# A graph network in three layers on one core: node parts stored by even and odd tiles, and the last group's store issued later

## The chip, the cores and the metric

The kernel runs on one core of one Trainium2 chip. The core has five engines with a queue of instructions each: PE multiplies matrices, DVE, ACT and POOL compute on vectors, SP issues transfers. SBUF is the on-chip memory of 128 partitions, PSUM takes the matmul results, DRAM is the memory outside. The metric is the device time of one execution in microseconds (us); where several runs are shown, their median.

## The reference

2,500 nodes carry 256 numbers each; 80,000 edges, sorted by `dst`, join them. The input is normalised row by row and clipped at zero, and then three edge convolutions follow, each

```python
m = concat([h[dst], h[src] - h[dst]]) @ W + b      # one row for each edge
s = segment_sum(m, dst); cnt = edges that end in the node
h = relu(s / max(cnt, 1))
```

The output is `x + concat([h0, h1, h2, h3]) @ Wf + bf`.

## The kernel before

The sum over edges is turned into a product with a matrix of counts. With `Wt` and `Wb` the upper and lower half of `W`, the sum for a node is `cnt * h @ (Wt - Wb)` plus the sum of `z = h @ Wb` over the sources of its edges. So each layer first makes `z`, 20 tiles of 128 nodes, and then multiplies it with the count matrix `a`, whose rows are source nodes and whose columns are destination nodes.

`z` is kept in two parts, `zh` (rounded to the matmul's fp32r format) and `zl` (the rest), so that two fast matmuls give the product nearly in fp32. Both lie in SBUF as `[128, 20, 256]`: tile `t` starts 1,024 bytes after tile `t - 1`, so all tiles of a part have the same address modulo 256. In the built program `zh` starts at byte 57504 and `zl` at byte 77984 of a partition, both 160 modulo 256.

The destinations are cut into five groups: four of 480 columns and one of 468 (`GWS`, in windows of 6). A group's slice of `a` is `[128, 20, n]` fp32r, in one of two buffers in turn (`apools`), at bytes 151200 and 189600, again 160 modulo 256. A row of 480 columns is 1,920 bytes, seven and a half times 256, so rows of even tiles start at 160 modulo 256 and rows of odd tiles at 32. A row of 468 columns is 1,872 bytes, so those starts move by 80 from tile to tile.

`layer(l, g, a, own)` is the inner loop. For each tile `i` it issues four matmuls: output half 0 with `zh` and `zl`, output half 1 with `zh` and `zl`. The 128 x 128 piece of `z` is the stationary operand (the weights, loaded anew for each matmul) and the row `a[:, i, :n]` is streamed. Four more matmuls add `hT` times `Wt - Wb` (L966).

Layer 0 (called with `PEo`, so its matmuls carry the helper's line L280) also builds `a`, group by group: DVE compares keys (`one_m`, `one_n`), PE counts, ACT copies the counts into the next group's `a`. Each of the first four groups is stored to DRAM by `store_a` (`finish`), as the later layers need it again. The fifth stays in SBUF for layer 1, and is stored after layer 1's nodes in the source text, but on the queue object `SP`, which leaves the place in SP's stream to the tile scheduler. `SPo`, `PEo`, `DVEo`, `ACTo` and `POOLo` are the same engines with program order kept. Layers 1 and 2 read the groups back with `load_a`; layer 1 walks the groups from the last to the first.

56 edges of the few nodes left over from the windows are not in `a`. Their rows of `z` are fetched from DRAM by indirect transfers that POOL issues: in layer 0 by `gather` (accumulating into `sums`), in later layers by `gather_pairs` (into spare buffers `one_m`, added by DVE). For this the nodes go to `z_dram`: in layer 0 by `keep_nodes`, `zh` first from SP, then `zl` added on from POOL, for five ranges of tiles; in later layers by `nodes_split`, tile by tile. `layer_few` closes each layer: it needs the sum of the fetched rows (`add_sums`).

`split_high`, `split_low` and `nodes_split` write `zh` and `zl`; `keep_nodes`, `layer` and `layer_few` read them.

Of the kernel before, what the change touches and what calls it, by code (L numbers as in the profile page):

```python
# [8 lines left out]
F32 = mybir.dt.float32  # L9
I32 = mybir.dt.int32  # L10
AF = mybir.ActivationFunctionType
OP = mybir.AluOpType
# [253 lines left out]
F32R = mybir.dt.float32r  # L266
# [45 lines left out]
def by_windows(ctx: ExitStack, tc: tile.TileContext, x, src, dst, Ws, bs, Wf, bf, out, missing):  # L312
    nc = tc.nc
    PE, DVE, ACT, POOL, SP = nc.tensor, nc.vector, nc.scalar, nc.gpsimd, nc.sync
    PEo, DVEo, POOLo, ACTo, SPo = (InOrder(tc, e) for e in (PE, DVE, POOL, ACT, SP))
    P = 128
    N, D = x.shape
    E = src.shape[0]
    NT = (N + P - 1) // P
# [9 lines left out]
    FEW = 112  # L329
# [18 lines left out]
    NG = len(GWS)  # L348
    Q = NT // 2
# [9 lines left out]
    const = ctx.enter_context(tc.tile_pool(name="const", bufs=1))  # L359
# [9 lines left out]
    def bank():  # L369
        return ps[-1].tile([P, 512], F32, name="bank")  # L370
# [1 line left out]

    acc = const.tile([P, NT, D], F32, name="acc")
    hT = const.tile([P, DC, NP], F32, name="hT")
    zh = const.tile([P, NT, D], F32R, name="zh")
    zl = const.tile([P, NT, D], F32R, name="zl")
    key_m = const.tile([P, NW, CH, REP], BF16, name="key_m")
    key_n = const.tile([P, NW, CH, REP], BF16, name="key_n")
    away = const.tile([P, WG, CAP], BF16, name="away")
# [16 lines left out]
    z_dram = [dram.tile([NP, D], F32, name=f"z_dram{l}") for l in range(L)]  # L396
# [3 lines left out]
    cnt_few = const.tile([P, FEW], F32R, name="cnt_few")  # L400
    mine = const.tile([P, W], F32, name="mine")
    most = const.tile([P, 1], F32, name="most")
    a_dram = [dram.tile([P, NT, n * W], F32, name=f"a_dram{g}") for g, n in enumerate(GWS)]
# [5 lines left out]

    shift = pp.tile([P, P + 1], F32, name="shift")  # L410
    ident = shift[:, :P]


    dst_rows = dst.rearrange("(p c) -> p c", p=P)
# [17 lines left out]
    def load_wb(l, queue=SP):  # L432
        ws[l] = wpool.tile([P, DC, D], F32, name="wt"), wpool.tile([P, DC, D], F32, name="wb", bufs=1)
        queue.dma_start(ws[l][1], Ws[l][D:2 * D, :].rearrange("(c p) d -> p c d", p=P))
# [29 lines left out]
    def load_b(l, queue=SP):  # L464
        queue.dma_start(brow[PAD:PAD + 1, l % 2, :], bs[l].rearrange("(o d) -> o d", o=1))
# [262 lines left out]
    zf0 = pp.tile([P, D], F32, name="zf0")  # L728
# [5 lines left out]
    def split_high(q):  # L734
        t, p = 2 * q, pz[q, False]
        if q == Q - 1:
            ACTo.copy(zh[:, t, :], p[:, :D])
            ACTo.copy(zh[:, t + 1, :], zf0)
        else:
            ACTo.copy(zh[:, t:t + 2, :], p.rearrange("p (i d) -> p i d", i=2))  # L740

    def split_low(q):
        t, p = 2 * q, pz.pop((q, False))
        if q == Q - 1:
            DVEo.tensor_sub(zl[:, t, :], p[:, :D], zh[:, t, :].bitcast(F32))
            DVEo.tensor_sub(zl[:, t + 1, :], zf0, zh[:, t + 1, :].bitcast(F32))
        else:
            DVEo.tensor_sub(zl[:, t:t + 2, :], p.rearrange("p (i d) -> p i d", i=2),
                            zh[:, t:t + 2, :].bitcast(F32))

    def first_final(q):
        ACTo.copy(acc[:, 2 * q:2 * q + 2, :], pz.pop((q, True)).rearrange("p (i d) -> p i d", i=2))
# [1 line left out]
    def nodes_split(l, t, zf):  # L754
        pz = bank()
        for c in range(DC):
            PE.matmul(pz[:, :D], hT[:, c, t * P:(t + 1) * P], ws[l][1][:, c, :],  # L757
                      start=(c == 0), stop=(c == DC - 1))
        sc = share[:, t:t + 1]
        if t == NT - 1:  # L760
            DVEo.scalar_tensor_tensor(zf, pz[:, :D], sc, brow[:, l % 2, :], op0=OP.mult, op1=OP.add)
        else:
            ACT.activation(zf, pz[:, :D], AF.Copy, scale=sc)
        SPo.dma_start(z_dram[l][t * P:(t + 1) * P, :], zf)
        DVEo.tensor_copy(zh[:, t, :], zf)
        DVEo.tensor_sub(zl[:, t, :], zf, zh[:, t, :].bitcast(F32))

    def add_rest(ts):

# [19 lines left out]
    def group_of(g):  # L789
        return FEW + sum(GWS[:g]) * W, GWS[g] * W  # L790

    def touched(g):
        c0, n = group_of(g)
        return [t for t in range(NT) if (t + 1) * P > c0 and t * P < c0 + n]

    def new_a(g):

        n = group_of(g)[1]
        a = apools[g % 2].tile([P, NT * GS], F32R, name="a")
        return a[:, :NT * n].rearrange("p (t n) -> p t n", n=n)  # L800
# [53 lines left out]
            store_a(g, a)  # L854
        yield

    def store_a(g, a):
        for t in range(0, NT, 5):
            SP.dma_start(a_dram[g][:, t:t + 5, :], a[:, t:t + 5, :].bitcast(F32))

    def load_a(g):
        a = new_a(g)
# [9 lines left out]

    def keep_nodes(l, a, b):

        to = z_dram[l][a * P:b * P, :].rearrange("(k p) d -> p k d", p=P)
        SPo.dma_start(to, zh[:, a:b, :].bitcast(F32))
        yield
        POOLo.dma_start(to, zl[:, a:b, :].bitcast(F32), accum_op=OP.add)

    def gather(l):  # L880

# [16 lines left out]
    def rooms(l):  # L898

        for _ in range(AHEAD):  # L900
            two = room()
            yield two[:, 0, :]
            yield two[:, 1, :]
        for i in range(SUMS):
            yield sums[:, i, :]
        for _ in range(AHEAD):
            yield hot.tile([P, BW * CH, NB], BF16, name="one_n", bufs=AHEAD).rearrange(
                "p k m -> p (k m)")[:, :2 * D].bitcast(F32)
# [24 lines left out]
    def layer_few(l):  # L933
        pa = ps_agg.tile([P, DC, 512], F32, name="pa")
        for o in range(DC):
            for c in range(DC):
                PEo.matmul(pa[:, o, :FEW], ws[l][0][:, c, o * P:(o + 1) * P], hT[:, c, :FEW],
                           start=(c == 0), stop=False)
            for z in (zh, zl):
                PEo.matmul(pa[:, o, :FEW], z[:, NT - 1, o * P:(o + 1) * P], cnt_few, start=False, stop=False)  # L940
            PEo.matmul(pa[:, o, :FEW], sums[:, 0, o * P:(o + 1) * P], only, start=False, stop=True)
        ACTo.activation(hT[:, :, :FEW], pa[:, :, :FEW], AF.Relu)

    unit = [None]

    def layer(l, g, a, own, PE=PE, ACT=ACT):

        c0, n = group_of(g)
        pa = ps_agg.tile([P, DC, 512], F32, name="pa")
        ways = [(o, c) for o in range(DC) for c in range(DC)]  # L950
        units = [(0, k) for k in range(NT)]
        for i, u in enumerate(own):
            units.insert(u + i, (1, i))
        last = {}
        for kind, i in units:
            last.update({o: (kind, i, o) for o in (range(DC) if kind == 0 else ways[i][:1])})
        for kind, i in units:
            if kind == 0:
                for o in range(DC):
                    for z in (zh, zl):  # L960
                        unit[0] = PE.matmul(pa[:, o, :n], z[:, i, o * P:(o + 1) * P], a[:, i, :n],  # L961
                                            start=(i == 0 and z is zh),
                                            stop=(z is zl and last[o] == (kind, i, o)))
            else:
                o, c = ways[i]
                unit[0] = PE.matmul(pa[:, o, :n], ws[l][0][:, c, o * P:(o + 1) * P], hT[:, c, c0:c0 + n],  # L966
                                    start=False, stop=(last[o] == (kind, i, o)))
            yield
        ACT.activation(hT[:, :, c0:c0 + n], pa[:, :, :n], AF.Relu)  # L969
# [8 lines left out]
    a = new_a(0)  # L978
# [55 lines left out]
    for g in range(NG):  # L1034
# [26 lines left out]
        if g + 1 < NG:  # L1061
            run(finish(g + 1, a1))
            held, a = a, a1
# [4 lines left out]
    tiles = {NG - 1: a, NG - 2: held}  # L1068
    for l in range(1, L):
        groups = list(range(NG))  # L1070
        if l % 2:
            groups.reverse()


        last = [t for t in touched(groups[0]) if t]
        for t, zf in zip([t for t in range(1, NT) if t not in last] + last + [0], rooms(l)):
            nodes_split(l, t, zf)
        if l == 1:

            store_a(NG - 1, tiles[NG - 1])  # L1080
        few = gather_pairs(l)
        next(few)
        if l + 1 < L:
            load_b(l + 1)
            load_wb(l + 1)
            load_wt(l + 1)
        finished = []
        for j, g in enumerate(groups):
            now = [t for t in touched(g) if t not in finished]
            for t in now:  # L1090
                final(l, t)
            finished += now
            rest = add_rest(now) if l == 1 else None
            if j == NG - 1:
                load_wf(l + 1)
            for u, _ in enumerate(layer(l, g, tiles[g], LATE)):
                if u % 4 == 1:
                    next(few, None)
                if rest and u in (1, NT):
                    next(rest, None)  # L1100
            if j == 1 and l + 1 < L:
                DVEo.tensor_sub(ws[l + 1][0], ws[l + 1][0], ws[l + 1][1])
            if j + 2 < NG:
                del tiles[g]
                tiles[groups[j + 2]] = load_a(groups[j + 2])
        run(few)
        add_sums(2)
        layer_few(l)
# [41 lines left out]
```

## Time and profile before

| | us |
|---|---|
| median of three runs | 512.57 (512.41 to 512.95) |
| the profiled execution | 510.9 |
| its span, first to last instruction | 509.1 |
| layer 0's matmuls with `a` | 61.0 to 199.9 |
| wait for the fetched rows, `layer_few` of layer 0 | PE idle 1.75 |
| layer 1's nodes begin | 206.8 |
| layer 2's nodes begin | 347.1 |
| last layer's output begins | 486.8 |

An engine's busy share is a mean over stages. Starts of matmuls are times at which the next one began, so the distance from one start to the next is what a matmul costs in a dense stream; the shown duration of one (some 0.38 us) overlaps the next.

### The profile page before, as it was taken

How to read it: one execution, taken by the hardware profiler on the slowest of the kernel's cores; microseconds unless marked ns; L12 is line 12 of the kernel's file. 1: busy time of each engine (PE TensorE's matmuls, PEld its weight loads, DVE VectorE, ACT ScalarE, POOL GpSimd, SP SyncE). 2: the span in 40 equal slices, each digit the busy share in tenths (PEclk: the TensorE clock that was granted, in tenths of full speed). 3: DMA queues.
4: the chain of work that ended last, by engine and by line, in shares of the span. 5: the costliest groups of instructions: out<-in, count | busy, mean ns of one | idle time of the engine just before them, and what ended most of it. 6: DMA issues, size and time to landing. Idle time of an engine off the chain costs nothing.

```text
span 509.1 us, 7543 instructions
## 1 busy us (share of the span) xinstructions
PE 498.3 (98%) x2875; PEld 410.4 (81%) x2875; DVE 262.4 (52%) x552; ACT 135.9 (27%) x310; POOL 250.2 (49%) x231
## 2 busy tenths in 40 slices
PE   8999999999999999899999999999999999999996
PEld 4898888778788887788687878788887878787885
DVE  7999988888897810782214240415812231213033
ACT  5676667744634310430000000004300000000010
POOL 3694218888888870007666573610176645451000
PEclk9999999999999999999999999999999999999999
DMA  9327987895959898343399999872335878898023
GB/s 277 95 71 135 227 275 242 281 232 163 324 87 363 124 169 306 112 138 94 114 379 338 300 242 285 82 131 85 123 106 196 354 242 279 236 257 84 1 89 119
DMA packets 41475, 98.72 MB, mean 194 GB/s; under 512 B 4999, under 2 KB 31574, under 8 KB 35798
## 3 DMA queue, kind: packets, MB, share of 16 engines
q1 hardware_dynamic: 22198, 68.78, 36.7%
q0 software_dynamic: 18304, 28.26, 32.5%
q10 hardware_dynamic: 928, 1.11, 0.7%
q8 instruction: 24, 0.39, 0.3%
q14 instruction: 21, 0.17, 0.1%
HBM read 60.63 MB, written 37.50 MB: 193 GB/s over the span
## 4 chain that ended last, share of the span: by engine, by line
PE 67%; POOL 19%; DMA 8%; issue 4%; DVE 1%; ACT 0%; DVEq 0%; POOLq 0%; SPq 0%; ACTq 0%
PE pa L961 34%; POOL sums L280 19%; PE bank L781 10%; PE bank L757 7%; PE pa L966 6%; PE pz L280 6%; DMA sums<-z_dram,who 3%; PE bank L280 2%; DMA wf<-in_L_gnn_Wf_dram 2%; DMA z_dram<-zl 1%; DMA z_dram<-zh 1%; PE pa L280 1%; DMA dst_i<-in_dst_dram 1%; PE turned L280 1%; DVE sums L280 0%
## 5 line engine op out<-in xcount | busy, mean ns | idle before, releaser
L280 POOL DMA_INDIRECT one_m<-z_dram,who x112 | 111.0, 991 | 153.2 <-DVE acc L280 40.5
L961 PE MATMUL pa<-a,zh 128*128 128x480 f32 (+1 forms) x400 | 152.8, 382 | 0.0
L961 PE MATMUL pa<-a,zl 128*128 128x480 f32 (+1 forms) x400 | 151.4, 378 | 0.0
L280 POOL DMA_INDIRECT sums<-z_dram,who x56 | 95.7, 1710 | 23.8 <-issue 16.8
L280 DVE TENSOR_TENSOR sums<-sums,one_m 128x512 f32<-128x512 f32 x52 | 36.0, 692 | 106.1 <-DMA one_m<-z_dram,who 104.2
L961 PEld LDWEIGHTS pa<-a,zl 128*128 128x128 f32 x400 | 75.1, 188 | 11.3
L961 PEld LDWEIGHTS pa<-a,zh 128*128 128x128 f32 x400 | 75.1, 188 | 11.0
L280 PE MATMUL pa<-a,zh 128*128 128x480 f32 (+1 forms) x200 | 81.5, 408 | 0.0
L280 DVE TENSOR_TENSOR one_m<-iota_m,key_m 128x1024 bf16<-128x1024 bf16 x100 | 68.6, 686 | 16.5 <-PE bank L280 14.4
L280 PE MATMUL pa<-a,zl 128*128 128x480 f32 (+1 forms) x200 | 75.7, 379 | 0.0
L969 ACT ACTIVATE hT<-pa 128x960 f32<-128x960 f32 (+1 forms) x10 | 9.7, 966 | 232.5 <-PE pa L966 205.0
L280 ACT CAST a<-bank 128x480 fp32r<-128x480 f32 x100 | 51.0, 564 | 59.1 <-PE bank L280 51.5
L280 DVE TENSOR_TENSOR one_n<-iota_n,key_n 128x960 bf16<-128x960 bf16 x100 | 65.0, 650 | 0.0
L280 DVE SCALAR_TENSOR_TENSOR acc<-bank,share,acc 128x256 f32<-128x256 f32 x60 | 28.7, 483 | 65.6 <-PE bank L781 59.1
L781 PE MATMUL bank<-wf,hT 128*128 128x256 f32 x240 | 54.0, 379 | 1.8 <-issue 1.3
L781 PEld LDWEIGHTS bank<-wf,hT 128*128 128x128 f32 x240 | 45.5, 190 | 11.4 <-issue 5.1
L280 PEld LDWEIGHTS <-one_m 128*128 128x128 bf16 x796 | 43.3, 98 | 8.6 <-issue 3.5
L280 PE MATMUL bank<-one_n,one_m 128*128 128x120 bf16 x796 | 48.9, 216 | 0.0
L280 PEld LDWEIGHTS pa<-a,zh 128*128 128x128 f32 x200 | 37.7, 188 | 8.4 <-issue 3.0
L280 PEld LDWEIGHTS pa<-a,zl 128*128 128x128 f32 x200 | 37.6, 188 | 7.0 <-issue 2.1
L757 PE MATMUL bank<-wb,hT 128*128 128x256 f32 x160 | 34.9, 379 | 0.0
L966 PE MATMUL pa<-hT,wt 128*128 128x480 f32 (+1 forms) x80 | 34.0, 565 | 0.1
(145 smaller groups left out, 413.1 us busy)
## 6 DMA issues: line engine op xcount, KB each, us to landing
a<-a_dram SPq DMA_DIRECT2D x20, 1200.0 KB
a_dram<-a SPq DMA_DIRECT2D x16, 1200.0 KB
a_dram<-a SPq DMA_DIRECT2D x4, 1170.0 KB
a<-a_dram SPq DMA_DIRECT2D x4, 1170.0 KB
out_dram<-acc SPq DMA_DIRECT2D x19, 128.0 KB
z_dram<-one_m SPq DMA_DIRECT2D x16, 128.0 KB
z_dram<-sums SPq DMA_DIRECT2D x16, 128.0 KB
acc<-in_x_dram POOLq DMA_DIRECT2D x4, 512.0 KB
```

The source lines that it names most:

```text
L280: return self.tc.keep_in_program_order(call(*args, **kwargs))
L757: PE.matmul(pz[:, :D], hT[:, c, t * P:(t + 1) * P], ws[l][1][:, c, :], start=(c == 0), stop=(c == DC - 1))
L781: PE.matmul(po[:, :D], hT[:, c, t * P:(t + 1) * P], wfs[l][:, c, :], start=(c == 0), stop=(c == DC - 1))
L961: unit[0] = PE.matmul(pa[:, o, :n], z[:, i, o * P:(o + 1) * P], a[:, i, :n], start=(i == 0 and z is zh), stop=(z is zl and last[o] == (kin ...
L966: unit[0] = PE.matmul(pa[:, o, :n], ws[l][0][:, c, o * P:(o + 1) * P], hT[:, c, c0:c0 + n], start=False, stop=(last[o] == (kind, i, o)))
L969: ACT.activation(hT[:, :, c0:c0 + n], pa[:, :, :n], AF.Relu)
```

## The change

Two edits.

`zh` and `zl` become `[128, 2, 2560 + 32]`: first the ten even tiles, then, after 32 floats (128 bytes) of room, the ten odd tiles. `tile_of` and `pair_of` find a tile, or tiles `2q` and `2q + 1`, in it. An even tile's weights start at 160 modulo 256 as before; an odd tile's start at 32. The tiles that follow in SBUF move by 512 bytes (`zl` by 256), which keeps them as they were modulo 256: the buffers of `a` start at 151712 and 190112. So in the groups of 480 columns the weights of a tile and the row that they are multiplied with start at the same address modulo 256, for even and for odd tiles. `keep_nodes` can't write both halves of a range in one transfer any more; ranges of more than two tiles go in two.

The store of the fifth group is issued on `SPo`, so that it stands in SP's stream where the text has it: behind the 20 node stores of layer 1 (the second of the three layers).

```diff
-    zh = const.tile([P, NT, D], F32R, name="zh")
-    zl = const.tile([P, NT, D], F32R, name="zl")
+    zh = const.tile([P, 2, Q * D + 32], F32R, name="zh")
+    zl = const.tile([P, 2, Q * D + 32], F32R, name="zl")
...
+    def tile_of(z, t):
+        return z[:, t % 2, t // 2 * D:(t // 2 + 1) * D]
+
+    def pair_of(z, q):
+        return z[:, :, q * D:(q + 1) * D]
...
     def split_high(q):
...
-            ACTo.copy(zh[:, t:t + 2, :], p.rearrange("p (i d) -> p i d", i=2))
+            ACTo.copy(pair_of(zh, q), p.rearrange("p (i d) -> p i d", i=2))
...
-        DVEo.tensor_copy(zh[:, t, :], zf)
-        DVEo.tensor_sub(zl[:, t, :], zf, zh[:, t, :].bitcast(F32))
+        DVEo.tensor_copy(tile_of(zh, t), zf)
+        DVEo.tensor_sub(tile_of(zl, t), zf, tile_of(zh, t).bitcast(F32))
...
-    def store_a(g, a):
+    def store_a(g, a, queue=SP):
         for t in range(0, NT, 5):
-            SP.dma_start(a_dram[g][:, t:t + 5, :], a[:, t:t + 5, :].bitcast(F32))
+            queue.dma_start(a_dram[g][:, t:t + 5, :], a[:, t:t + 5, :].bitcast(F32))
...
     def keep_nodes(l, a, b):
 
-        to = z_dram[l][a * P:b * P, :].rearrange("(k p) d -> p k d", p=P)
-        SPo.dma_start(to, zh[:, a:b, :].bitcast(F32))
+        to = z_dram[l][a * P:b * P, :].rearrange("(q i p) d -> p i q d", i=2, p=P)
+        ways = [(slice(0, 2), 0)] if b - a == 2 else [(i, slice(None)) for i in range(2)]
+
+        def tiles_of(z):
+            return z[:, :, a // 2 * D:b // 2 * D].bitcast(F32).rearrange("p i (q d) -> p i q d", d=D)
+
+        for i, q in ways:
+            SPo.dma_start(to[:, i, q, :], tiles_of(zh)[:, i, q, :])
         yield
-        POOLo.dma_start(to, zl[:, a:b, :].bitcast(F32), accum_op=OP.add)
+        for i, q in ways:
+            POOLo.dma_start(to[:, i, q, :], tiles_of(zl)[:, i, q, :], accum_op=OP.add)
...
-                PEo.matmul(pa[:, o, :FEW], z[:, NT - 1, o * P:(o + 1) * P], cnt_few, start=False, stop=False)
+                PEo.matmul(pa[:, o, :FEW], tile_of(z, NT - 1)[:, o * P:(o + 1) * P], cnt_few, start=False, stop=False)
...
-                        unit[0] = PE.matmul(pa[:, o, :n], z[:, i, o * P:(o + 1) * P], a[:, i, :n],
+                        unit[0] = PE.matmul(pa[:, o, :n], tile_of(z, i)[:, o * P:(o + 1) * P], a[:, i, :n],
...
-            store_a(NG - 1, tiles[NG - 1])
+            store_a(NG - 1, tiles[NG - 1], SPo)
```

More of the change, by code (lines that the diff above doesn't have):

```diff
@@ L736, in split_high @@
         if q == Q - 1:
-            ACTo.copy(zh[:, t, :], p[:, :D])
-            ACTo.copy(zh[:, t + 1, :], zf0)
+            ACTo.copy(tile_of(zh, t), p[:, :D])
+            ACTo.copy(tile_of(zh, t + 1), zf0)
         else:
-            ACTo.copy(zh[:, t:t + 2, :], p.rearrange("p (i d) -> p i d", i=2))
+            ACTo.copy(pair_of(zh, q), p.rearrange("p (i d) -> p i d", i=2))
     def split_low(q):
@@ L744, in split_low @@
         if q == Q - 1:
-            DVEo.tensor_sub(zl[:, t, :], p[:, :D], zh[:, t, :].bitcast(F32))
-            DVEo.tensor_sub(zl[:, t + 1, :], zf0, zh[:, t + 1, :].bitcast(F32))
-        else:
-            DVEo.tensor_sub(zl[:, t:t + 2, :], p.rearrange("p (i d) -> p i d", i=2),
-                            zh[:, t:t + 2, :].bitcast(F32))
+            DVEo.tensor_sub(tile_of(zl, t), p[:, :D], tile_of(zh, t).bitcast(F32))
+            DVEo.tensor_sub(tile_of(zl, t + 1), zf0, tile_of(zh, t + 1).bitcast(F32))
+        else:
+            DVEo.tensor_sub(pair_of(zl, q), p.rearrange("p (i d) -> p i d", i=2), pair_of(zh, q).bitcast(F32))
     def first_final(q):
```

## The prediction

> **What bounds the kernel now.** I read the page first (busy shares and the chain of waits), then the chain in order of time around the border of layer 0 and layer 1, then busy times by windows there, and last the timeline of PE inside a group.
>
> ```profile
> PE 498.3 (98%) x2875; PEld 410.4 (81%) x2875; DVE 262.4 (52%) x552; ACT 135.9 (27%) x310; POOL 250.2 (49%) x231
> PE 67%; POOL 19%; DMA 8%; issue 4%; DVE 1%; ACT 0%; DVEq 0%; POOLq 0%; SPq 0%; ACTq 0%
> ```
>
> PE is busy for 98% of the span: time falls only where a matmul gets shorter or one of PE's few pauses goes. POOL's 19% and DMA's 8% in the chain are layer 0's fetches. PE works beside them, so they count only for the pause at their end:
>
> ```profile
> 187.23 15.51 DMA sums<-z_dram,who
> 203.12 1.24 DVE sums L280
> 205.59 1.37 PE pa L280 x10
> 206.95 17.28 PE bank L757 x80
> ```
>
> The columns are start, length, and what. The last fetch, issued at 187.23, lands 15.5 us later; three additions follow, and only then can PE close layer 0. PE's last matmul without the sums ends at 203.84 (timeline), so it is idle for 1.75 us. Why so late a landing is in the windows (time of the window, then PE, PEld, DVE, ACT, POOL busy with counts, clock, DMA share, GB/s):
>
> ```profile
> 184.00:188.00 4.00, 4.00 (x20) 3.55 (x20) 0.72 (x5) 0.00 (x0) 3.39 (x3) 1.00 1.06 155
> 188.00:192.00 4.00, 4.00 (x20) 3.54 (x20) 0.00 (x0) 0.00 (x0) 0.77 (x1) 1.00 1.06 379
> 192.00:196.00 4.00, 4.00 (x21) 3.55 (x20) 0.00 (x0) 0.00 (x0) 0.00 (x0) 1.00 1.05 374
> 196.00:200.00 4.00, 4.00 (x21) 3.53 (x20) 0.00 (x0) 0.00 (x0) 0.00 (x0) 1.00 1.06 372
> 200.00:204.00 4.00, 3.83 (x15) 2.08 (x13) 0.88 (x1) 0.74 (x1) 0.00 (x0) 1.00 0.39 116
> 204.00:208.00 4.00, 2.41 (x16) 2.29 (x17) 2.06 (x4) 0.70 (x3) 0.00 (x0) 1.00 0.09 13
> ```
>
> From 188 to 200 the transfer engines are full at some 375 GB/s although POOL has stopped issuing. That is the fifth group's store: 4.7 MB from about 185 to 202. Counted in the packet records, the fetches pass some 93 packets per us at 182 to 184 and only 27 to 50 per us beside the store.
>
> The other place is the matmul stream. Layers 1 and 2 spend 34% of the chain on L961:
>
> ```profile
> 278.35 0.38 PE L961 MATMUL pa<-a,zh 128*128 128x480 f32 x1
> 278.57 0.38 PE L961 MATMUL pa<-a,zl 128*128 128x480 f32 x1
> 278.79 0.39 PE L961 MATMUL pa<-a,zh 128*128 128x480 f32 x1
> 279.01 0.39 PE L961 MATMUL pa<-a,zl 128*128 128x480 f32 x1
> 279.24 0.37 PE L961 MATMUL pa<-a,zh 128*128 128x480 f32 x1
> 279.45 0.38 PE L961 MATMUL pa<-a,zl 128*128 128x480 f32 x1
> 279.66 0.38 PE L961 MATMUL pa<-a,zh 128*128 128x480 f32 x1
> 279.87 0.38 PE L961 MATMUL pa<-a,zl 128*128 128x480 f32 x1
> 280.09 0.38 PE L961 MATMUL pa<-a,zh 128*128 128x480 f32 x1
> ```
>
> The first four rows are tile 2 of a group (an even one), the next four tile 3. Start to start the even tile takes 0.89 us, the odd one 0.85. In the start records to the nanosecond the intervals are 217, 220, 222, 224 in even tiles and 210, 213, 213, 213 in odd ones, the same in all eight groups of 480 columns of layers 1 and 2, with one stall apart. They repeat every two tiles (3,840 bytes, 15 times 256), not every four, so it is the address modulo 256 that shows. Means: even 220.8, odd 212.7, all 216.5 ns.
>
> [...]
>
> **Part 1, the store.** Removed from about 185 to 202: 4.7 MB beside the fetches. At 187.23 some 560 packets of theirs are left (27 to 50 per us until 202). At the 93 per us seen just before they need 6 us, so they land at about 193.5. The additions (2.4 us) end at 196, eight before PE asks for them at 203.84. The pause of 1.75 us goes, and PE's own stream is late next. Gain 1.75 us; bounds 0 (the fetches do not speed up) and 1.75 (nothing else is late there).
>
> The store's four issues (some 0.4 us each) now stand on SP behind the last node store, at 225.6. Behind them on SP stands the reload of group 2, issued at 251.74 before. At 372 GB/s the store needs 12.6 us, with the fetches between 17: over by 238 to 243. Layer 1's first group reads the buffer until 245.3 anyway, so the reload waits no longer. The store also meets layer 1's fetches (from 228.98). At the disturbed rate these lose some 10 us. Four pairs of buffers are out at once, and POOL later stands idle for PE's progress, 5.98 us at 270.16 and 2.38 at 320.29, so the lag is caught up. The layer's last fetched row is added at 341.3, PE asks at 345.9: 4.6 us of cover. Without it, each us of lag beyond that would cost a us. I take 0.
>
> **Part 2, `keep_nodes`.** Four more issues on SP and four on POOL (1.2 to 1.3 us each there). POOL has pauses of 9.63 and 9.97 us before its issues at 54.57 and 68.06; the two earliest extra ones fall into the first, the others end by 60. The last range (8, 10), which the fetches wait for, stays one transfer. SP's extra issues stand before the first store of `a` at 58.49 with pauses between. Cost 0; if the cover fails, up to 5 us later fetches, which meet the 8 us just won. ACT's and DVE's writes of `zh` and `zl` keep their size: 0.
>
> **Part 3, addresses.** Row and weights now agree for even and odd tiles; before, even tiles agreed and odd ones were 128 apart. It concerns 640 matmuls of layers 1 and 2 (mean 216.5 ns) and the 288 of layer 0 that run without counts between them (mean 218.6). Groups of 468 columns see all distances before and after (mean 211.9): 0. What interval 480 columns settle on when every tile agrees, the trace does not show, as agreement never lasts longer than one tile. Read plainly, agreement is the costlier side, 220.8. But the interval has a memory. It climbs inside an even tile. A group's first tile, also agreeing, runs at 215, 212, 217. In layer 0 after an interruption odd tiles run at 220, 220, 220 and even ones at 219, 216, 218 (means there 218.9 even, 218.4 odd). So the distance alone does not set it. The bounds are the lowest and highest interval seen, 205 and 226. I take no change of the mean, the middle of the two steady values seen (213.3 and 220): cost 0. Each ns moves 640 + 288 = 0.93 us.
>
> Sum: 509.1 - 1.75 = 507.35 span, 510.9 - 1.75 = 509.15 for the profiled execution. The median of the runs lies 1.67 above that execution; the same step from 512.57 gives 510.8. An unexplained pause of 1.25 us in PE near 250 may come or go in a single execution.
>
> **Rivals.** About 0.2%, 1.0 us, is what a measurement can tell here.
>
> Agreement makes matmuls shorter (faster). For it: 215, 212, 217 in a fresh tile, and 205 to 207 where 468 columns happen to fit. Against it: even tiles are the longer ones. At 213.3: 640 x 3.2 + 288 x 5.3 = 3.6 us, with the store 5.3, so 507.2; at 206: 6.7 + 3.6 + 1.75, so 500.5.
>
> Agreement makes them longer (the other side, slower): the weight load and the row start in the same place of 256 bytes in every tile, and nothing resets the climb. For it: even against odd in eight groups. Against it: the memory above. At 220.8: 640 x 4.3 + 288 x 2.2 = 3.4, less 1.75, so 514.2; at 225: 518. It outweighs the store from 1.9 ns per matmul on, and can be measured from 3.0 ns, a mean of 219.5.
>
> The store does not do what it says: the fetches alone keep the engines full (share 1.14 from 180 to 184 at 81 GB/s) and land as late, or layer 1's fetches end too late. 512.6 to 514.
>
> **How the numbers follow.** Forecast (store gained, addresses about even, own range 509.5 to 512.0) 0.36; agreement shorter 0.33; agreement longer 0.23; store without gain 0.08. Faster: 0.33 and most of the forecast, 0.64. Slower: most of the third case and a little of the last, 0.19. The rest, 0.17, is no change. The range leaves out the far ends of the shorter case (below 504) and of the longer one (above 514.5). The likeliest case gives 510.8.
>
> **What would show it.** Store: the last fetch of layer 0 lands before 196, no pause of PE ahead of `layer_few`, 4.7 MB on SP's queue from 226 to 243, no new pause before 345.9. Addresses: starts of the L961 matmuls, four in even and four in odd tiles; 866 ns per tile is the forecast, 853 the shorter case, 883 the longer one. I am wrong if odd and even tiles still differ, or if layer 0 ends late for another reason.

## The result, and the profile after

| | before | after |
|---|---|---|
| median, us | 512.49 (509.81 to 512.95, 4 runs) | 506.15 (506.01 to 506.40, 4 runs) |
| profiled execution, us | 510.9 | 506.01 |
| its span, us | 509.1 | 504.2 |

The ratio is 0.9888, with a 95% interval of 0.9853 to 0.9922. The change takes 6.3 us off the median, where the prediction had 1.8 (512.6 to 510.8). In the two profiled executions the difference is 4.9 us.

The page of the kernel after, busy shares and the shares of the chain:

```profile
PE 496.4 (98%) x2875; PEld 410.4 (81%) x2875; DVE 262.4 (52%) x552; ACT 135.4 (27%) x310; POOL 253.6 (50%) x235
PE 96%; DMA 2%; DVE 0%; SPq 0%; ACT 0%; issue 0%; ACTq 0%
```

POOL's 19% and DMA's 8% are gone from the chain: the end no longer hangs on layer 0's fetches. The chain in order of time after, at the border of layer 0 and layer 1 (start, length, what), shows it:

```profile
183.08 21.25 PE pa L280 x100
204.32 17.28 PE bank L763 x80
221.61 4.32 PE bank L787 x20
```

Before, this stretch went from POOL to a transfer to DVE and only then to PE; now PE follows PE. Why, is in the windows of the kernel after (window, length, then PE, PEld, DVE, ACT, POOL busy, clock, DMA share, GB/s):

```profile
188.00:192.00 4.00, 4.00 (x20) 3.55 (x19) 0.00 (x0) 0.00 (x0) 0.10 (x1) 1.00 1.10 81
192.00:196.00 4.00, 4.00 (x20) 3.52 (x19) 1.70 (x2) 0.00 (x0) 0.00 (x0) 1.00 0.32 31
196.00:200.00 4.00, 4.00 (x19) 3.23 (x18) 1.25 (x3) 0.00 (x0) 0.00 (x0) 1.00 0.00 0
200.00:204.00 4.00, 4.00 (x22) 2.75 (x21) 0.00 (x0) 0.95 (x1) 0.00 (x0) 1.00 0.00 0
```

Beside the store these windows moved 372 to 379 GB/s; now they move 81, then 31, then nothing. From the packet records the last fetch lands at 193.90 (202.40 before), DVE's additions are done at 196.7, and PE asks for the sums at 203.00. The store itself is issued on SP at 223.07, and its packets run until 239. PE at the matmul that reads the sums, two rows of before and two of after (start, shown duration, what; in brackets the idle time ahead and its releaser):

```profile
203.56 0.27 PE L280 MATMUL pa<-cnt_few,zl 128*128 128x112 f32 x1
205.59 0.47 PE L280 MATMUL pa<-only,sums 128*128 128x112 f32 x2 [1.75 <-DVE sums L280]
202.89 0.28 PE L280 MATMUL pa<-cnt_few,zl 128*128 128x112 f32 x1
203.00 0.43 PE L280 MATMUL pa<-only,sums 128*128 128x112 f32 x2
```

From start to start this step took 2.03 us before and takes 0.11 now, so the wait cost 1.9 us, some 0.2 more than the idle time shown.

The matmul stream of the kernel after, one even tile (the first four rows) and one odd tile (the next four) in a group of 480 columns of layer 1 (start, shown duration, what):

```profile
277.66 0.38 PE L974 MATMUL pa<-a,zh 128*128 128x480 f32 x1
277.87 0.38 PE L974 MATMUL pa<-a,zl 128*128 128x480 f32 x1
278.09 0.37 PE L974 MATMUL pa<-a,zh 128*128 128x480 f32 x1
278.31 0.38 PE L974 MATMUL pa<-a,zl 128*128 128x480 f32 x1
278.52 0.38 PE L974 MATMUL pa<-a,zh 128*128 128x480 f32 x1
278.74 0.38 PE L974 MATMUL pa<-a,zl 128*128 128x480 f32 x1
278.96 0.37 PE L974 MATMUL pa<-a,zh 128*128 128x480 f32 x1
279.17 0.38 PE L974 MATMUL pa<-a,zl 128*128 128x480 f32 x1
279.39 0.38 PE L974 MATMUL pa<-a,zh 128*128 128x480 f32 x1
```

Even and odd tiles now take the same time: 0.86 and 0.87 us, 1.73 for both. Before it was 0.89 and 0.85, 1.74 for both. In the groups of 480 columns of layers 1 and 2 the layout did what it says and moved almost nothing. The two fp32r matmuls with `zh` and `zl` together take 0.43 us; one of 480 columns in fp32 (`hT` times `Wt - Wb`) is two records 402 ns apart, 0.80 us.

Where the 4.9 us of the two profiled executions come from, followed by the starts of the stages: layer 0's first matmul with `a` begins 0.2 us earlier; layer 1's nodes begin 2.63 us earlier (206.79 to 204.16), which is 1.9 for the wait, the 0.2 from the start and some 0.5 in layer 0's matmuls; layer 1's second group begins 4.18 us earlier (252.46 to 248.28), as a pause of PE near 250 is gone; after another place, near 386, it is 4.87. The rest of the stream is the same length. The pause near 250, in the kernel before:

```profile
250.17 0.59 PE L781 MATMUL bank<-wf,hT 128*128 128x256 f32 x2 [0.44 <-issue]
251.57 0.81 PE L781 MATMUL bank<-wf,hT 128*128 128x256 f32 x3 [0.81 <-issue]
```

"issue" means that nothing in the profile released it. Two things in this have to be settled: whether these two pauses belong to the change, and why the medians lie 6.3 apart.

### The profile page after: what moved, and what is told of

It reads as the page before. It is cut to its first block, busy times and chain, and to the rows that moved or that the text cites. A ratio compares the mean times of both kernels' runs of the same rounds, so it can differ in the third digit from the quotient of the medians.

```text
span 504.2 us, 7558 instructions
## 1 busy us (share of the span) xinstructions
PE 496.4 (98%) x2875; PEld 410.4 (81%) x2875; DVE 262.4 (52%) x552; ACT 135.4 (27%) x310; POOL 253.6 (50%) x235
## 4 chain that ended last, share of the span: by engine, by line
PE 96%; DMA 2%; DVE 0%; SPq 0%; ACT 0%; issue 0%; ACTq 0%
PE pa L974 34%; PE pa L280 22%; PE bank L787 10%; PE bank L280 9%; PE bank L763 7%; PE pz L280 7%; PE pa L979 6%; DMA wf<-in_L_gnn_Wf_dram 2%; PE turned L280 1%; DMA dst_i<-in_dst_dram 1%; DVE acc L280 0%; SPq L280 0%; ACT hT L280 0%; DVE first L280 0%; ACTq L280 0%
## 5 line engine op out<-in xcount | busy, mean ns | idle before, releaser
L280 POOL DMA_INDIRECT one_m<-z_dram,who x112 | 109.8, 980 | 149.4 <-DVE acc L280 73.5
## 6 DMA issues: line engine op xcount, KB each, us to landing
acc<-in_x_dram POOLq DMA_DIRECT2D x4, 512.0 KB, 11.6
```

The lines of the kernel that those rows point to most:

```text
L280: return self.tc.keep_in_program_order(call(*args, **kwargs))
```

## The experiments

The theory at this point: the store carries the gain, the wait that it removes costs more than its idle time, and the layout is worth a few tenths at most. The rivals: the layout carries what goes beyond the wait's 1.75 us; or the rest is chance in the profile of before. Letters for theories hold within the set of runs that names them.

### The two kernels again, and each edit alone

Four kernels on one chip, where before measured 510.65 (39 runs). First the kernel before, without an edit:

> The kernel before, once more with a profile. The profile on record has two pauses of PE that nothing in the program explains: 1.5 us near 249 (end of layer 1's first group) and 0.6 us near 386 (end of layer 2's first group). Theory A, the pauses come by chance from execution to execution: they stand elsewhere or are gone here, and the times spread over 509 to 513. Theory B, they belong to the order of work of the kernel before: they stand at the same two places again, with the same length within 0.3 us, and the span is 509.1 within 0.4.

Measured 510.89 (20 runs), ratio 1.0004 (0.9987 to 1.0022). Its profile has no pause near 250 nor near 386, so those come and go with the execution. But it shows something that the first profile of this kernel did not have. Windows of this run, the columns as above:

```profile
202.00:204.00 2.00, 1.70 (x9) 1.02 (x7) 0.53 (x1) 0.88 (x1) 0.00 (x0) 1.00 0.08 17
204.00:206.00 2.00, 0.07 (x1) 0.07 (x1) 1.93 (x4) 0.08 (x1) 0.00 (x0) 1.00 0.00 0
206.00:208.00 2.00, 2.00 (x10) 2.00 (x11) 0.48 (x1) 0.00 (x0) 0.00 (x0) 0.50 0.00 0
208.00:210.00 2.00, 2.00 (x8) 1.72 (x8) 0.00 (x0) 0.49 (x2) 0.00 (x0) 0.65 0.37 131
210.00:212.00 2.00, 2.00 (x11) 1.77 (x10) 1.38 (x4) 1.22 (x3) 0.00 (x0) 1.00 0.19 66
```

Read the clock, the third number from the right. PE waited from 203.70 to 205.93:

```profile
205.93 0.75 PE L280 MATMUL pa<-only,sums 128*128 128x112 f32 x2 [2.23 <-DVE sums L280]
```

Directly behind the wait its granted clock is a half, for 3.413 us by the clock record (the trace's list of stretches with one granted clock). The first node matmuls are 453, 427 and 390 ns apart, where most are 216. The thirteen intervals from the matmul that waited onward take 3.52 us here and 1.87 in the first profile of this kernel, which has the full clock there. So the half clock costs some 1.7 us, half of 3.413, on top of the wait. The store's price was therefore not the wait alone. Over the 59 executions of this kernel in this batch, the mean clock sorts the times: 21 with 0.997 and more have a median of 509.32, 35 with 0.994 to 0.996 one of 511.15, and three with 0.992 one of 514.28. One half-clock stretch of 3.413 us in 509 lowers the mean by 0.003. The last 0 to 2.7 us of a profiled execution are at half clock too (none in the first profile of the changed kernel, 0.93 us in that of the kernel before, in a later one of the changed kernel from 501.79 to its end at 504.47, a mean of 0.997), so a mean down to 0.997 needs no stretch inside the kernel, and single executions at 0.997 can't be told for certain.

Then the store alone, with the old addresses:

```diff
-    def store_a(g, a):
+    def store_a(g, a, queue=SP):
...
-            store_a(NG - 1, tiles[NG - 1])
+            store_a(NG - 1, tiles[NG - 1], SPo)
```

> The kernel before with the fifth group's store on SPo alone; addresses as before. Theory A (store gives 1.75 us and no more, the unexplained pauses are chance): last fetch of layer 0 lands at about 193, no wait ahead of layer_few, layer 1's nodes 1.75 us earlier than before, 0.3 to 0.4% less time than before. Theory B (the moved store also takes away the pause near 249, since SP's stream at that place is another): 1.75 + 1.5 us, 0.6 to 0.7% less. Intervals of the 480 column matmuls 220.8 in even and 212.7 in odd tiles, as before.

Measured 506.59 (506.51 to 506.87, 4 runs), ratio 0.9910 (0.9874 to 0.9945). The last fetch lands at 195.75, there is no wait, and the clock is full behind it. The groups of layers 1 and 2 keep 16.89 us from their second matmul to the last. So the store alone brings 4.06 us on this chip, more than either theory expected (1.75, or 3.25 with the pause near 250). The wait of 2.23 us cost 2.40 from start to start; with 1.7 for one half-clock stretch behind it that is 4.1, the gain on the median.

The layout alone, with the store left to the scheduler:

```diff
-            store_a(NG - 1, tiles[NG - 1], SPo)
+            store_a(NG - 1, tiles[NG - 1])
```

> The changed kernel with the fifth group's store on SP as before; addresses agree. Theory A (agreement gives 866 ns per tile in even and odd tiles, mean unchanged): layers 1 and 2 cost the same as before, layer 0's groups are 0.6 to 0.9 us shorter in all, the wait ahead of layer_few grows by as much, so no gain beyond 0.1%, apart from pauses that come by chance. Theory B (the layout takes away the pauses near 249 and 386): 2 us, 0.4% less than before.

Measured 509.06 (507.73 to 511.72, 20 runs), ratio 0.9977 (0.9960 to 0.9994). The fetches land at 202.67 and PE waits 2.40 us, as in the kernel before. The groups take 16.87 us in layers 1 and 2 (16.89 before), and the four large ones of layer 0 25.59, 29.74, 29.35 and 28.81 (25.78, 29.89, 29.40, 28.91 in the run of before beside it): 0.49 us less in layer 0, some 0.16 over the eight groups later. The median gained more than that, 1.6 us against 510.65. Among executions with a clock of 0.997 and more it is only 0.5 us (508.80 against 509.32), among those with 0.994 to 0.996 0.7 (510.45 against 511.15). The rest comes from fewer half clocks: 7 of 20 executions are under 0.997 here, 38 of 59 in the kernel before. Why fewer isn't shown; theory A had no gain beyond 0.1% here.

The changed kernel, without an edit:

> The changed kernel once more on the same chip, to be set against the two halves. Theory A (pauses by chance): 504.2 us of span plus a pause of up to 2 us somewhere in some executions; the gains of the two halves add up to that of the whole within 0.3%. Theory B (the pauses belong to the kernel before): span 504.2 within 0.4, no pause near 249 or 386.

Measured 506.77 (506.29 to 506.94, 4 runs), ratio 0.9912 (0.9877 to 0.9947). With the store alone at 506.59, the layout's part on top of the store isn't visible here; without a wait there is no half clock left for it to save.

### Filling the wait

If the half clock comes from PE's idling, work in the wait should prevent it. The kernel before, with eight bf16 matmuls of 512 columns ahead of the one that waits:

```diff
+            if l == 0 and o == 0:
+                spare = bank()
+                for _ in range(8):
+                    PEo.matmul(spare, ident_b, key_m.rearrange("p n j r -> p (n j r)")[:, :512], start=True, stop=True)
             PEo.matmul(pa[:, o, :FEW], sums[:, 0, o * P:(o + 1) * P], only, start=False, stop=True)
```

> The kernel before with eight bf16 matmuls of 512 columns into a spare PSUM buffer (about 1.7 us), placed in layer 0's layer_few just ahead of the matmul that waits for the fetched rows. Store and addresses as before. They add work that no output uses. Theory A (the wait costs twice: its own 1.8 to 2.4 us, and in more than half of the executions PE's clock falls to one half for 3.4 us behind it, worth 1.7 to 2 us): the wait stays, but PE isn't idle in it, so the clock stays whole; times come together at 508.5 to 510, median about 509.2, 1.5 us (0.3%) under the kernel before. Theory B (the scatter has another cause, such as transfers): median 510.7 and spread 508.5 to 514 as before, or 1.7 us more.

Measured 515.01 (513.70 to 517.91, 12 runs), ratio 1.0013 (0.9983 to 1.0043), on a chip where before measured 514.84. No gain, and the experiment is inconclusive. In its profiled execution PE had lost time at 88 to 94, so the fetches had landed (200.43) before it came to the fill, and the fill stood in the way of work. PE in order of time there (start, duration, what):

```profile
207.48 0.27 PE L280 MATMUL pa<-cnt_few,zl 128*128 128x112 f32 x1
207.83 1.67 PE L280 MATMUL bank<-key_m,ident_b 128*128 128x512 bf16 x7
209.34 0.37 PE L280 MATMUL pa<-only,sums 128*128 128x112 f32 x2
```

Seven of the eight are in the trace. The fill costs some 1.8 us (207.48 to 209.34, where 0.11 would do) whenever the wait is short. The lowest times say the same: 513.70 against 511.79 for before. Of the executions 7 in 12 have a mean clock of 0.997 or more, and 12 in 37 of before; that points the right way, but is too few to show it.

### Other distances

In these three kernels every tile has one and the same distance between row and weights, as in the changed kernel, but it is 128, 64 or 192 bytes modulo 256 instead of none. The parts are read at an offset `SH` of 32, 48 or 16 floats in a larger tile:

```diff
-    zh = const.tile([P, 2, Q * D + 32], F32R, name="zh")
-    zl = const.tile([P, 2, Q * D + 32], F32R, name="zl")
+    zh, zl = (const.tile([P, 2 * (Q * D + 32) + 64], F32R, name=n)[:, SH:SH + 2 * (Q * D + 32)].rearrange(
+        "p (i x) -> p i x", i=2) for n in ("zh", "zl"))
```

> The changed kernel with all weights of z moved by 128 bytes more, so that weights and row are 128 apart modulo 256 in even and odd tiles. Theory A (a steady distance always ends in a mean of about 216.5 ns): 866 ns per tile, the time of the changed kernel within 0.1%. Theory B (128 apart is where the odd tiles of before stood, 213.3 ns): 853 ns per tile, 0.26 us per group, 2.1 us in layers 1 and 2 and up to 1.5 in layer 0, so 0.4 to 0.7% less than the changed kernel, 503.3 to 504.8.

> As the run with 128, but rows 64 bytes ahead of the weights modulo 256 in all tiles. Theory A (any steady distance gives about 216.5 ns): 866 ns per tile. Theory B (the distance sets the interval): another value than at 0 and at 128; each ns per matmul is worth 0.64 us in layers 1 and 2.

> As the run with 128, but rows 192 bytes ahead of the weights modulo 256 in all tiles. Theory A: 866 ns per tile. Theory B: another value than at 0 and at 128.

| distance modulo 256 | group of 480, second to last matmul, us | ratio to before |
|---|---|---|
| 0 and 128 in turn (before) | 16.89 | |
| 0 (after) | 16.87 | 0.9888 (0.9853 to 0.9922), another batch |
| 64 | 16.91 | 0.9901 (0.9876 to 0.9927) |
| 128 | 16.97 | 0.9906 (0.9882 to 0.9930) |
| 192 | 16.84 | 0.9892 (0.9839 to 0.9944) |

From the best to the worst it is 0.13 us per group, 1.0 us over the eight groups. And the interval isn't a function of the distance: odd tiles, 128 apart, ran at 213 ns beside even ones at 221, but when all tiles are 128 apart the mean is higher than before, not lower (870 ns per tile, where theory B had 853). What sets the interval remains open; that agreement would make the stream clearly faster or slower is excluded. The 192 bytes gain 0.03 us per group, 0.2 us in all, on the changed kernel's groups; that is below what the times can tell, so no kernel here is shown to beat the changed one.

The first of these profiles also shows a pause that no semaphore and no transfer explains. PE of the kernel with 128 bytes, in order of time (in brackets the idle time ahead and its releaser):

```profile
381.96 0.47 PE L974 MATMUL pa<-a,zh 128*128 128x480 f32 x1
384.07 0.38 PE L974 MATMUL pa<-a,zl 128*128 128x480 f32 x1 [1.64 <-issue]
384.77 0.37 PE L974 MATMUL pa<-a,zh 128*128 128x480 f32 x1 [0.32 <-issue]
```

Here too the clock is a half for 3.413 us behind it, from 385.9 on. The fetching of instructions, an obvious suspect, doesn't show as the releaser: the transfers of instructions around this pause run from 359.8 to 360.9 and from 386.7 to 387.9.

### A wait made to measure

The wait of before can't be taken away without moving the store, but the changed kernel can be given one. VectorE copies a piece of the last eviction of layer 0 to an unused place and then runs one or four identity operations over `sums`, so that the few matmuls wait, whose rows have long been there. The node matmuls keep program order, so that nothing slips ahead of the wait. The long one:

```diff
-            PE.matmul(pz[:, :D], hT[:, c, t * P:(t + 1) * P], ws[l][1][:, c, :],
+            PEo.matmul(pz[:, :D], hT[:, c, t * P:(t + 1) * P], ws[l][1][:, c, :],
...
+    DVEo.tensor_copy(sums[:, 1, :], hT[:, 0, group_of(NG - 1)[0]:][:, :D])
+    for _ in range(4):
+        DVEo.tensor_tensor(sums[:, 0, :], sums[:, 0, :], sums[:, 0, :], op=OP.max)
     layer_few(0)
```

Beside them on the same chip ran the changed kernel and the store alone once more; before measured 512.82 there.

> The changed kernel once more, as the yardstick for the three kernels beside it on this chip. Every theory expects no wait ahead of the few matmuls of layer 0, a last fetch landed near 194 us, and a group of 480 columns of 16.87 us from its second matmul to its last; ratio to before of 0.987 to 0.991.

> The store moved, the old addresses. If the layout is worth nothing but the 0.05 to 0.19 us per group of layer 0 that its kernel alone showed, it is 0.2 to 0.6 us slower than the changed kernel beside it. If the layout is worth 1 us or more, it is that much slower. If the layout costs something, it is faster than the changed kernel.

> The changed kernel, with one copy and one identity operation on VectorE between the last eviction of layer 0 and the few matmuls that read sums, so that TensorE waits there although the fetches landed long before: estimated 1.4 us of pause (eviction ends at 203.5, then 0.3 and 0.43 us, while PE asks at 203.0). Theory A (a pause of 2 us and more lets the clock fall to a half for 3.4 us in a part of the executions, a shorter one doesn't): time of the changed kernel beside it plus 1.4, no half clock behind the pause. Theory B (a pause costs its own length, whatever it is; the half clock has other causes): plus 1.4 as well. Theory C (any pause, however short, is doubled): plus 2.8 or more.

> The same with four identity operations: estimated 2.7 us of pause. Theory A: plus 2.7 in some executions and plus 4.4 (2.7 and half of 3.413) in the others, so two heaps of times, a median of plus 2.7 to 4.4 against the changed kernel, mean clocks of 0.996 or less where the time is long, and in the profile, if it falls among the long ones, a half clock directly behind the pause. Theory B: plus 2.7 in all executions, no heaps, clock 0.999 to 1.0. Theory C: plus 5 or more.

| | median, us | ratio to before | wait in the profile, us | executions with a mean clock under 0.997 |
|---|---|---|---|---|
| changed kernel | 506.45 (506.20 to 507.02) | 0.9888 (0.9859 to 0.9916) | none | 0 of 6 |
| store alone | 507.74 (507.44 to 508.40) | 0.9912 (0.9883 to 0.9940) | none | 0 of 6 |
| short wait | 507.88 (507.28 to 508.33) | 0.9913 (0.9884 to 0.9941) | 1.09 | 0 of 6 |
| long wait | 511.07 (508.96 to 513.03) | 0.9962 (0.9943 to 0.9981) | 2.47 | 15 of 22 |
| before | 512.82 (509.70 to 516.79) | | | 18 of 27 |

PE of the kernel with the long wait, in order of time:

```profile
203.51 0.27 PE L280 MATMUL pa<-cnt_few,zl 128*128 128x112 f32 x1
206.25 0.47 PE L280 MATMUL pa<-only,sums 128*128 128x112 f32 x2 [2.47 <-DVE sums L280]
```

The wait is there, released by DVE as made. Its 22 times lie in three heaps: seven executions with a clock of 0.997 and more at a median of 509.26, ten with 0.994 to 0.996 at 511.08, five with 0.992 at 512.37. Against 506.45 that is 2.8 us, which is the wait; 4.6 us, the wait and one half-clock stretch; and 5.9, where the mean clock of 0.992 points to a second stretch. The profile is of an execution of the first heap, with no half clock inside, so in this kernel the place of the half clock behind the wait is inferred from times and mean clocks; it is seen in the repeated kernel before. The short wait costs 1.4 us and leaves the clock alone. Theory A holds, B and C fall: the wait of 2.47 us has, in 15 of 22 executions by their mean clock, a second price that the one of 1.09 us had in none of 6.

Which executions it hits fits the phase of a clock record: the borders of its stretches are whole multiples of 3.413 us apart (the full clock lasts 501.759 us in the first profile of the kernel before and 498.346 in that of the changed kernel, 147 and 146 of them). Laying this grid over the waits: in the repeated kernel before the whole 2.23 us fell between two borders, and the half clock follows at the next one. In the long wait's profiled execution 1.79 us fell in one stretch and 0.68 in the next, with no half clock; in the layout-alone run 0.73 and 1.67, with none. The whole waits (2.23, 2.47 and 2.40 us) don't sort these three; the longest idle time between two borders does, 2.23 us with a half clock, 1.79 and 1.67 without. That is a fit to three waits, not a test, and what makes the clock fall isn't shown. The unexplained pauses don't sort so cleanly: in the kernel with 128 bytes 1.9 us were followed by a half clock, but in the filled kernel so were 1.5 and 1.6 us between two borders. There several idle pieces lie among matmuls whose ends are modelled, so the true idle time may be longer than the sum. What sets the grid's phase wasn't tried.

The store alone is 1.3 us behind the changed kernel in this batch, and was 0.2 ahead in the first. Its profile here has the two unexplained losses again, some 0.4 us between the first two groups of layer 0 and 0.66 near 386, where the changed kernel's profile beside it has none. From the first matmul of layer 0's first group to that of layer 2's last group, the profiles without any such pause say 398.84 us for the store alone and 398.30 for the changed kernel: 0.5 us for the layout.

One thing stays open in this batch. Its executions of the kernel before at full clock (0.997 and more, 9 of 27) have a median of 511.50, 3.8 us above the store alone, where a wait as profiled elsewhere costs 1.9 to 2.6 from start to start. The rest isn't explained; no profile of the kernel before was taken on this chip.

## Why the prediction was right or wrong

**The fetches and the store: right.** Landing at 193.5 was forecast and 193.90 measured, by the packet rate alone. (The 560 packets left out the small ones, which the 93 per us include; counted alike some 630 were left, 6.8 us, 194.0.) The store was to be over by 238 to 243, and was at 239. Nothing in layer 1 waited for it: the last addition ends at 337.5, and PE asks at 341.5, a cover of 4.1 us where 4.6 was forecast.

**`keep_nodes`: right.** The four more issues on POOL are seen in its count (231 to 235), and the first fetch starts at 75.50, not later than before (76.28).

**Addresses: right for layers 1 and 2, small for layer 0.** 866 ns per tile was forecast, and 865 measured. The rivals needed 853 or 883. In layer 0 the forecast was zero, and 0.5 us was gained there, in the four groups that are interrupted by counting.

**The term that was mis-sized is the pause.** The prediction wrote "Gain 1.75 us; bounds 0 (the fetches do not speed up) and 1.75 (nothing else is late there)". The upper bound was wrong. It took the pause for its idle time in one profiled execution, in which the idle time had fallen on both sides of a border of the clock's grid (0.56 and 1.19 us) and no half clock followed. In the three profiles with this wait (two of the kernel before, one of the layout alone) it is 1.75, 2.23 and 2.40 us, its cost in time some 0.2 more than the idle time shown, and by the mean clock 38 of 59 executions have at least one half-clock stretch, worth 1.7 us. On the first experiment chip the store alone is worth 4.06 us on the median. The prediction put no clock into its sum. Its profile couldn't show the need: there the clock is full from 6.4 us to 508.2. The repeated run of the same kernel, with 2.23 us of wait, has 3.413 us at half clock behind it.

**The step from the profile to the median failed too.** "The median of the runs lies 1.67 above that execution; the same step" was carried over to the changed kernel. That step was not an offset: the changed kernel's profiled execution is 506.01 and its median 506.15. Half clocks and pauses in the median executions of before are the likely content of the 1.67 us; the clocks of those executions are not on record, so this is argued. The profiled execution, 510.9, stood 1.5 us under the lowest of the three runs; that was a sign that something in the kernel was decided by chance.

**The pauses near 250 and 386.** The prediction left the one near 250 to chance. That holds: repeated runs of the same kernel have or lack it. The 4.9 us between the two first profiles contain 2.2 us of these pauses, which this does not show to be owed to the change. Their cause was not found. The 6.3 us between the medians are therefore explained in part: wait 1.9 to 2.6, one half clock 1.7 and layout 0.5 make 4.1 to 4.8, and the rest is about the size of the pauses. None of the three profiles of the changed kernel has such a pause, and its 14 executions in three batches lie between 506.01 and 507.02; but the kernel with the short wait, which has the same layout and store, shows 0.7 us of them near 386. Whether the change makes them rarer is open.

The measured time lies where the prediction had put "agreement shorter" (507.2 with the store). It came there by another way: in the main the store, not the addresses. The forecast's own range (509.5 to 512.0) was missed. That the measured time lies inside the whole one (504 to 514.5) is luck: the room below 509.5 was made for shorter matmuls, and these did not come.

## What to carry to other kernels

In this kernel a wait of TensorE with 1.75 us of idle time, in an otherwise dense stream, cost 1.92 us from start to start, and one with 2.23 cost 2.40. A half clock behind it, worth 1.7 us, came on top in one profile. By the mean clock, 38 of 59 executions of the kernel before, 7 of 20 of the layout alone and 15 of 22 of the long wait had one (waits of 1.75 to 2.47 us in their profiles), and none of 6 with the wait of 1.09 us. Look at the spread of the runs and at each execution's mean clock before taking one profile's wait as the size of the gain: with the wait the spread went as well, from 509.70 to 516.79 us in 27 executions to 506.20 to 507.02 in 6 beside them. A transfer that nobody needs soon should be issued after those that somebody waits for, in an order that is written out: beside the store the fetches moved 27 to 50 packets per us, without it 82 to 96.

## What the hardware showed that was not expected

- The half clock came for 3.413 us after a wait with 2.23 us of idle time inside one period of that length, and not after waits with 1.79 or 1.67; after pauses it came with sums of 1.5, 1.6 and 1.9 us. None of the 30 executions of the changed kernel, the store alone and the short wait, in three batches, went below a mean clock of 0.997.
- The streamed matmuls of 480 columns take 210 to 226 ns each, in patterns that change with where row and weights start modulo 256 (220.8 ns in even and 212.7 in odd tiles before, 0.86 and 0.87 us per tile after) and that settle over several tiles (in the changed kernel up to 226 ns in the second and third tile of a group, 212 to 221 from the fourth on), with means between 216 and 218 ns at the four distances and in the kernel before.
- TensorE pauses in some executions without a releaser: from start to start 2.11 and 0.70 us near 382 to 385 with 128 bytes, 0.70 near 386 and 0.82 and 1.18 near 250 in the first profile of the kernel before. They return at the same places: the one near 386, between its 2354th and 2362nd matmul, is in seven of fourteen profiles. The place is tied to the program, the occurrence to chance and perhaps to the chip: it is in all four profiles of one chip and in none of the four of another. It matters as these pauses, too, were followed by a half clock in two profiles.
